# Window attention in a fused Swin and Fourier kernel: the transpose of the attention weights done by VectorE in 32x32 blocks, with the off-diagonal blocks exchanged by SBUF transfers

## The chip, the core and the metric

The kernel runs on one core of a Trainium2 chip. The core has TensorE (PE, matrix multiplies; its weight loads are shown apart as PEld), VectorE (DVE), ScalarE (ACT), GpSimd (POOL) and SyncE (SP), which here only issues DMAs. Each engine works through its own instructions in order and waits on semaphores for the others. The metric is the device time in microseconds from the first to the last instruction. All data are float32.

## What is computed

The input is 32 images of 56 x 56 tokens with 128 channels. Two residual layers follow each other, each behind a group norm (32 groups of 4 channels over the whole image):

```python
x = x + _L0_conv_ref(_gn(x), rpb_table, w_qkv, w_proj, b_proj)   # shifted-window attention
x = x + _L1_conv_ref(_gn(x), w0, w1, W1, b1, W2, b2)             # DCT mixing, then a feed-forward
```

The change lies in the first. The image is rolled by 3 in both directions and cut into 8 x 8 windows of 7 x 7 = 49 tokens. Each window has 4 heads of 32 channels:

```python
attn = jnp.einsum('bhid,bhjd->bhij', q, k)
attn = attn + bias[None]                                    # relative position bias
attn = attn.reshape(B, nW, NH, N, N) + mask[None, :, None]  # shift mask, 0 or -100
attn = jax.nn.softmax(attn.reshape(-1, NH, N, N), axis=-1)
out = jnp.einsum('bhij,bhjd->bihd', attn, v).reshape(-1, N, C)
out = out @ w_proj.T + b_proj
```

The second layer takes a cosine transform along the width and along the height (32 modes each), mixes channels for each mode, transforms back, adds the two, and runs a feed-forward of 128 to 512 to 128 with a relu.

## The kernel before

**Rows.** The unit of work of the attention is a row of 8 windows (7 x 56 tokens); an image has 8 rows, the run has 256. Two windows lie side by side on the 128 partitions, at 0 to 48 and 64 to 112 (JP = 64, WT = 49), so a row has NP = 4 pairs of windows. The score tile `a` holds [128, head, pair, column] for one row; its columns are padded from 49 to 64, and three such tiles rotate.

**What happens to a row.** In its own cycle (a cycle is one pass of the main loop, one row started per cycle): `attn_qk` makes queries and keys, `attn_scores` the scores (TensorE, then VectorE adds bias and mask into `a`, L439), `attn_max` takes the maximum per query (VectorE L449) and subtracts it (GpSimd L450), `attn_v` makes the values, `attn_exp` is the exponential (ScalarE L456), `attn_divide` sums (VectorE L461), takes the reciprocal (L463) and multiplies (GpSimd L464). The weights are now [query, key]; for the product with the values they are needed as [key, query]. `attn_transpose` does that on TensorE against an identity matrix: per pair of pairs and head one transpose of 113 x 113 (PW = 64 + 49 columns hold two windows, so that the result holds the same window pair turned, with columns of other pairs beside it), eight per row, into two PSUM banks; VectorE evacuates one (L485) and ScalarE the other (L483) into tiles `aT`. Three cycles after its own, `attn_values` multiplies with the values (L500, 32 small matmuls), and ScalarE (L533) and VectorE (L531) add the bias while they write `oT`; `attn_project` applies the output weights, VectorE adds the residual (L548), and SP stores the row to a scratch image in DRAM (L554). `attn_sums` prepares the second norm (squares on ScalarE, L570, sums on VectorE).

**Order of work.** TensorE, ScalarE, VectorE and GpSimd follow the order of the program as it is written (a manual schedule); SP's order is laid out by the framework. The main loop lets rows of the attention alternate with the second layer of earlier images: `halves_first` (queries and keys, first half of a feed-forward group), `half_columns` (transforms and mixing), `eighths` (values of row c-3), `quarters` (scores of row c, transforms back), then `attn_max` and `full`, then `halves_last` (values of row c, second half of the feed-forward group, exponential and division of row c, projection of row c-3). `full` transposes in even cycles only, rows c-2 and c-1 together. In even cycles the max of row c stands between these two on VectorE, in odd cycles it stands alone:

```python
for k in (2, 1) if cycle % 2 == 0 else ():
    im, i = row(cycle - k)
    if im:
        attn_transpose(im, i, cycle - k)
    if k == 2 and row(cycle)[0]:
        attn_max(cycle)
next_groups(cycle)
```

In one cycle of eight (row 6 of an image) `next_groups` prepares the next image: 28 transposes on TensorE, and on GpSimd eight additions of a bias (L307) that stand between that row's subtraction and its multiplication. The image's norm (`image_norm`, L334 to L361) follows on VectorE.

**Buffers.** The attention uses four PSUM banks in rotation (`pa`), the second layer four others (`pc`). Tile `res` (two buffers) carries the residual of a feed-forward group: loaded from the scratch image (L745), given its bias on GpSimd (L752), added on VectorE (L788) and stored to the output (L808). Tile `z` (three buffers) takes mixed modes to DRAM (L690), tile `zT` brings them back turned (L701), and `htok` brings columns of the scratch image (L668). Tile `sq` holds the squares and has one buffer of its own.

## Time and profile before

| | |
|---|---|
| timed runs | 3606.96, 3611.10, 3613.36 us (median 3611.1) |
| profiled execution | 3611.8 us, mean granted TensorE clock 0.997 |
| matmuls | 72192, of which 2048 are the transposes of the attention |
| DMA | 390.30 MB, mean 108 GB/s; the queue of SP keeps the 16 DMA engines 39.0% busy |

In the lines of the profile shown below, a group of instructions reads: line of the kernel, engine, operation, output <- inputs, shapes, count | busy time in us, mean ns of one | idle time of its engine just before, and what ended it. Lines of the order of time read: start in us, length in us, engine, line, operation, count, and in brackets the idle time before it with its releaser. PE is TensorE, DVE VectorE, ACT ScalarE, POOL GpSimd, SPq the queue of SP. L112 is the helper through which most matmuls are issued.

### The profile page before, as it was taken

How to read it: one execution, taken by the hardware profiler on the slowest of the kernel's cores; microseconds unless marked ns; L12 is line 12 of the kernel's file. 1: busy time of each engine (PE TensorE's matmuls, PEld its weight loads, DVE VectorE, ACT ScalarE, POOL GpSimd, SP SyncE). 2: the span in 40 equal slices, each digit the busy share in tenths (PEclk: the TensorE clock that was granted, in tenths of full speed). 3: DMA queues.
4: the chain of work that ended last, by engine and by line, in shares of the span. 5: the costliest groups of instructions: out<-in, count | busy, mean ns of one | idle time of the engine just before them, and what ended most of it. 6: DMA issues, size and time to landing. Idle time of an engine off the chain costs nothing.

```text
span 3611.8 us, 161664 instructions
## 1 busy us (share of the span) xinstructions
PE 3552.9 (98%) x72192; PEld 2827.2 (78%) x72192; DVE 2251.9 (62%) x4722; ACT 2145.5 (59%) x4044; POOL 1375.3 (38%) x1437
## 2 busy tenths in 40 slices
PE   7899999999999999999999999999999999999999
PEld 5678787777777787877777787877877878777776
DVE  7766666665666666666656666666666666666641
ACT  5555566665666655666556666556665566655553
POOL 5443343433443433434333434343443344342421
PEclk9999999999999999999999999999999999999999
DMA  4334433444434444343444344443444443444343
GB/s 118 92 102 112 115 106 101 109 112 110 111 98 115 109 109 120 97 110 106 114 106 115 95 111 112 112 117 93 112 108 115 108 112 95 114 109 114 94 115 99
DMA packets 687349, 390.30 MB, mean 108 GB/s; under 512 B 39967, under 2 KB 657600, under 8 KB 686400
## 3 DMA queue, kind: packets, MB, share of 16 engines
q1 hardware_dynamic: 686045, 379.65, 39.0%
q8 instruction: 568, 9.31, 1.1%
q14 instruction: 125, 1.02, 0.1%
q10 hardware_dynamic: 611, 0.32, 0.0%
HBM read 218.29 MB, written 161.48 MB: 105 GB/s over the span
## 4 chain that ended last, share of the span: by engine, by line
PE 93%; DVE 4%; ACT 1%; issue 1%; POOL 1%; DMA 0%; SPq 0%; ACTq 0%; POOLq 0%; DVEq 0%
PE pc L112 38%; PE pa L112 15%; PE pa L409 6%; PE pc L680 6%; PE pa L475 6%; PE pc L646 6%; PE pa L431 5%; PE pa L500 4%; PE pc L719 4%; PE pa L276 1%; PE pc L276 1%; DVE a L439 1%; DVE xf L730 0%; DVE oT L531 0%; POOL rstd L617 0%
## 5 line engine op out<-in xcount | busy, mean ns | idle before, releaser
L450 POOL TENSOR_TENSOR a<-a,mx 128x784 f32<-128x784 f32 x256 | 389.7, 1522 | 1390.7 <-DVE mx L449 966.6
L112 PE MATMUL pc<-wff,hid 128*64 128x128 f32 x12544 | 740.5, 273 | 1.3 <-ACT hid L764 1.0
L112 PE MATMUL pc<-xf,wff 128*64 128x512 f32 (+2 forms) x3584 | 718.3, 539 | 1.1 <-DVE xf L730 1.0
L112 PEld LDWEIGHTS pc<-wff,hid 128*64 128x64 f32 x12544 | 702.7, 137 | 8.0 <-ACT hid L764 4.6
L461 DVE TENSOR_REDUCE sm<-a 128x16 f32<-128x784 f32 x256 | 248.3, 970 | 675.7 <-ACT a L456 669.4
L464 POOL TENSOR_TENSOR a<-a,rs 128x784 f32<-128x784 f32 x256 | 389.6, 1522 | 606.8 <-DVE rs L463 549.4
L764 ACT ACTIVATE hid<-pc,b1sb 128x512 f32<-128x512 f32 (+2 forms) x896 | 522.6, 631 | 71.9 <-PE pc L112 68.9
L112 PEld LDWEIGHTS pc<-xf,wff 128*64 128x64 f32 x3584 | 276.3, 137 | 358.3 <-issue 239.0
L380 ACT ACTIVATE q<-pa,bqkv 128x392 f32<-128x392 f32 x256 | 150.4, 588 | 465.6 <-PE pa L112 459.8
L112 PE MATMUL pa<-xw,wn 128*64 128x392 f32 (+1 forms) x2048 | 390.2, 496 | 10.0 <-ACT wn L364 8.4
L531 DVE TENSOR_SCALAR oT<-pa,bqkv 128x98 f32<-128x98 f32 (+2 forms) x768 | 171.3, 278 | 241.6 <-PE pa L500 241.5
L456 ACT ACTIVATE a<-a 128x784 f32<-128x784 f32 x256 | 222.7, 870 | 146.6 <-POOL a L450 144.6
L752 POOL TENSOR_TENSOR res<-res,b2sb 128x512 f32<-128x512 f32 (+2 forms) x256 | 264.5, 1038 | 113.1 <-DMA res<-scr 105.0
L416 ACT COPY v<-pa 128x512 f32<-128x512 f32 x256 | 151.2, 591 | 244.5 <-PE pa L409 244.3
L307 POOL TENSOR_TENSOR xl<-xl,bproj 112x512 f32<-112x512 f32 (+1 forms) x256 | 287.1, 1143 | 0.0
L409 PE MATMUL pa<-wn,xw 128*64 128x128 f32 x4096 | 283.5, 280 | 3.4 <-ACT oT L533 1.6
L500 PEld LDWEIGHTS pa<-aT,v 49*32 49x32 f32 x16384 | 172.2, 105 | 145.7 <-issue 119.7
L439 DVE TENSOR_TENSOR a<-pa,bm 128x392 f32<-128x392 f32 x512 | 265.0, 560 | 25.8 <-PE pa L431 2.1
L483 ACT COPY aT<-pa 113x452 f32<-113x452 f32 x256 | 139.7, 546 | 208.3 <-PE pa L475 204.7
L449 DVE TENSOR_REDUCE mx<-a 128x16 f32<-128x784 f32 x256 | 246.5, 963 | 4.3
L409 PEld LDWEIGHTS pa<-wn,xw 128*64 128x64 f32 x4096 | 221.0, 137 | 36.0 <-issue 3.1
L788 DVE TENSOR_TENSOR res<-pc,res 128x512 f32<-128x512 f32 (+3 forms) x257 | 138.6, 550 | 175.4 <-PE pc L112 132.8
(97 smaller groups left out, 5746.3 us busy)
## 6 DMA issues: line engine op xcount, KB each, us to landing
zscr<-z SPq DMA_DIRECT2D x512, 112.0 KB
htok<-scr SPq DMA_DIRECT2D x256, 196.0 KB
zT<-zscr SPq DMA_DIRECT2D x192, 256.0 KB
res<-scr SPq DMA_DIRECT2D x160, 256.0 KB
out_dram<-res SPq DMA_DIRECT2D x160, 256.0 KB
scr<-xl SPq DMA_DIRECT2D x128, 224.0 KB
xl<-in_x_dram SPq DMA_DIRECT2D x32, 784.0 KB
xl<-in_x_dram SPq DMA_DIRECT2D x32, 672.0 KB
```

The lines of the kernel that those rows point to most:

```text
L112: nc.tensor.matmul(dst[ps], lhsT=lhsT[:, ps], rhs=rhs, start=start, stop=stop)
L307: nc.gpsimd.tensor_tensor(piece, piece, bproj.unsqueeze(1).to_broadcast([TC, e - a, C]), ALU.add)
L409: nc.tensor.matmul(pv[hs, j * C : (j + 1) * C], lhsT=im.xw[i][:, w * WT : w * WT + JP], rhs=im.w[:, 2 * C : 3 * C], start=True, stop=True,)
L439: nc.vector.tensor_tensor(a[:, 2 * hp : 2 * hp + 2, :, 0:WT].rearrange("p u w j -> p w u j"), ps[hp][:, :RT].rearrange("p (w u j) -> p w u ...
L449: nc.vector.tensor_reduce(mx, a3, axis=AX.X, op=ALU.max)
L450: nc.gpsimd.tensor_tensor(a3, a3, mx.unsqueeze(2).to_broadcast([P, 2 * NWR, WT]), ALU.subtract)
L456: nc.scalar.activation(a3, a3, AF.Exp)
L461: nc.vector.tensor_reduce(sm, a3, axis=AX.X, op=ALU.add)
L464: nc.gpsimd.tensor_tensor(a3, a3, rs.unsqueeze(2).to_broadcast([P, 2 * NWR, WT]), ALU.mult)
L500: nc.tensor.matmul(po4[u][h * HD : (h + 1) * HD, 2 * f + e], lhsT=v[ks, 2 * f + e, h * HD : (h + 1) * HD], rhs=im.aT[i][f][ks, h, e * JP : ...
L752: nc.gpsimd.tensor_tensor(res[:m, c0:c1], res[:m, c0:c1], b2sb[:m].unsqueeze(1).to_broadcast([m, c1 - c0, C]), ALU.add,)
L764: nc.scalar.activation(hf[:, :n], ph[:, :n], AF.Relu, bias=b1sb[:, f : f + 1])
```

## The change

The transposes on TensorE, their two PSUM banks per row and the two evacuations are gone. Instead:

- The score tiles are dense (49 columns, not 64), and two rotate instead of three.
- `attn_divide` multiplies the row twice, once into `own_sb` and once into `off_sb`, each with its 49 columns cut into two blocks: 0 to 31, and 32 to 48 in a block of 32. These are four GpSimd instructions over 128 x 512, 128 x 272, 128 x 512 and 128 x 272 elements. Both tiles exist once.
- Four DMAs from SP then copy, within each window's 64 partitions, the off-diagonal blocks of `off_sb` over those of `own_sb`: second block of the first 32 partitions from the first block of the second 32, and the other way round (32 partitions x 2 KB each).
- `attn_transpose` is one VectorE instruction per row that turns every 32 x 32 block of `own_sb` in place of its partitions and writes `eT` (128 x 1024 elements, two buffers). With the blocks exchanged, that is the whole transpose.
- In the main loop the max of row c stands first in every cycle, then the transpose of row c-1 follows on VectorE, then `next_groups`. Rows are no longer transposed in twos.
- `attn_values` reads `eT`; the windows are numbered so that a pair is two neighbours, and the pieces written to `oT` are runs of 7 tokens instead of 14 with the same number of elements.
- `sq` has no buffer of its own any more and takes one of the three of `z`.

In SP's order the four exchange DMAs of a row stand ahead of that cycle's last store of the output, the store of the row and the load of the next feed-forward group.

```diff
@@ -41,7 +41,7 @@
 QS = HD ** (-0.5)
 FF_GROUPS = (HB, HB, HB, HB, HB, 320, 256)
 FF_AT = (8, 9, 10, 12, 13, 14, 15)
-PW = JP + WT
+KB = 32
 CONV_BEGIN = NWR + 3
@@ -241,11 +241,12 @@
         nc.vector.memset(heads[h * HD : (h + 1) * HD, h % 2 : h % 2 + 1], 1.0)
     q_sb = big.tile([P, RT + JP - WT], F32, tag="q", name="q")
     nc.gpsimd.memset(q_sb, 0.0)
-    v_sb, a_sb = [], []
-    for i in range(3):
-        v_sb.append(big.tile([P, NWR // 2, C], F32, tag=f"v{i}", name=f"v{i}"))
-        a_sb.append(big.tile([P, NH, NP, JP], F32, tag=f"a{i}", name=f"a{i}"))
-        nc.gpsimd.memset(a_sb[i], 0.0)
+    v_sb = [big.tile([P, NP, C], F32, tag=f"v{i}", name=f"v{i}") for i in range(3)]
+    a_sb = [big.tile([P, NH, NP, WT], F32, tag=f"a{i}", name=f"a{i}") for i in range(2)]
+    own_sb = big.tile([P, 2, NH * NP, KB], F32, tag="own_blocks", name="own_blocks")
+    off_sb = big.tile([P, 2, NH * NP, KB], F32, tag="off_blocks", name="off_blocks")
+    nc.gpsimd.memset(own_sb, 0.0)
+    nc.gpsimd.memset(off_sb, 0.0)
@@ -258,7 +259,7 @@
         im.b = b
         im.half = b not in xls
         im.x = load_image(b, 1) if im.half else xls.pop(b)
-        im.xw, im.aT = {}, {}
+        im.xw, im.eT = {}, {}
         im.st = small.tile([P, NWR, 6], F32, tag="st0", name="st0", bufs=2)
         im.part = small.tile([TC, 2, C // 4, NWR], F32, tag="part", name="part", bufs=1)
         im.scr = dram.tile([S, S, C], F32, tag="scr", name="scr", bufs=2)
@@ -403,9 +404,9 @@
         pv = attn_bank()
 
 
-        for w in (0, 2, 1, 3, 4, 6, 5, 7):
-            hs = HALVES[w // 2 % 2]
-            j = w // 4 * 2 + w % 2
+        for w in range(NWR):
+            hs = HALVES[w % 2]
+            j = w // 2
             nc.tensor.matmul(
                 pv[hs, j * C : (j + 1) * C],
                 lhsT=im.xw[i][:, w * WT : w * WT + JP],
@@ -417,7 +418,7 @@
 
     def attn_scores(im, i, r):
 
-        q, a = q_sb, a_sb[r % 3]
+        q, a = q_sb, a_sb[r % 2]
@@ -444,7 +445,7 @@
             )
 
     def attn_max(r):
-        a3 = a_sb[r % 3].rearrange("p t w j -> p (t w) j")[:, :, 0:WT]
+        a3 = a_sb[r % 2].rearrange("p t w j -> p (t w) j")
         mx = small.tile([P, 2 * NWR], F32, tag="mx", name="mx")
         nc.vector.tensor_reduce(mx, a3, axis=AX.X, op=ALU.max)
         nc.gpsimd.tensor_tensor(
@@ -452,38 +453,33 @@
         )
 
     def attn_exp(r):
-        a3 = a_sb[r % 3].rearrange("p t w j -> p (t w) j")[:, :, 0:WT]
-        nc.scalar.activation(a3, a3, AF.Exp)
+        a2 = a_sb[r % 2].rearrange("p t w j -> p (t w j)")
+        nc.scalar.activation(a2, a2, AF.Exp)
 
     def attn_divide(r):
-        a3 = a_sb[r % 3].rearrange("p t w j -> p (t w) j")[:, :, 0:WT]
+        a3 = a_sb[r % 2].rearrange("p t w j -> p (t w) j")
         sm = small.tile([P, 2 * NWR], F32, tag="sm", name="sm")
         nc.vector.tensor_reduce(sm, a3, axis=AX.X, op=ALU.add)
         rs = small.tile([P, 2 * NWR], F32, tag="rs", name="rs")
         nc.vector.reciprocal(rs, sm)
-        nc.gpsimd.tensor_tensor(
-            a3, a3, rs.unsqueeze(2).to_broadcast([P, 2 * NWR, WT]), ALU.mult
-        )
-
-    def attn_transpose(im, i, r):
-
-        a = a_sb[r % 3]
-        im.aT[i] = []
-        for hf in range(2):
-            pt = attn_bank()
-            for h in range(NH):
-                nc.tensor.transpose(
-                    pt[:PW, h * P : h * P + PW],
-                    a[:PW, h, 2 * hf : 2 * hf + 2].rearrange("p w j -> p (w j)")[:, :PW],
-                    ident[:PW, :PW],
+        for dst in (off_sb, own_sb):
+            for k, (j0, n) in enumerate(((0, KB), (KB, WT - KB))):
+                nc.gpsimd.tensor_tensor(
+                    dst[:, k, :, :n],
+                    a3[:, :, j0 : j0 + n],
+                    rs.unsqueeze(2).to_broadcast([P, 2 * NWR, n]),
+                    ALU.mult,
                 )
-            aT = work.tile([P, 4, P], F32, tag="aT", name="aT", bufs=4)
-            src = pt[:PW].rearrange("p (m x) -> p m x", x=P)[:, :, :PW]
-            if hf:
-                nc.scalar.copy(aT[:PW, :, :PW], src)
-            else:
-                nc.vector.tensor_copy(aT[:PW, :, :PW], src)
-            im.aT[i].append(aT)
+        for p in range(0, P, JP):
+            lo, hi = slice(p, p + KB), slice(p + KB, p + JP)
+            nc.sync.dma_start(own_sb[lo, 1], off_sb[hi, 0])
+            nc.sync.dma_start(own_sb[hi, 0], off_sb[lo, 1])
+
+    def attn_transpose(im, i):
+
+        eT = work.tile([P, NH * NP, JP], F32, tag="eT", name="eT")
+        nc.vector.transpose(eT.rearrange("p t (k j) -> p k t j", k=2), own_sb)
+        im.eT[i] = eT
 
     def attn_values(im, i, r):
@@ -492,18 +488,18 @@
         po = [attn_bank(), attn_bank()]
         HALF = RT // 2
         po4 = [p[:, :HALF].rearrange("p (r n s) -> p n r s", r=WS, s=WS) for p in po]
-        for f in range(2):
-            for e in range(2):
-                for h in range(NH):
-                    for u in range(2):
-                        ks = slice(u * JP, u * JP + WT)
-                        nc.tensor.matmul(
-                            po4[u][h * HD : (h + 1) * HD, 2 * f + e],
-                            lhsT=v[ks, 2 * f + e, h * HD : (h + 1) * HD],
-                            rhs=im.aT[i][f][ks, h, e * JP : e * JP + WT],
-                            start=True,
-                            stop=True,
-                        )
+        eT = im.eT.pop(i)
+        for pr in range(NP):
+            for h in range(NH):
+                for u in range(2):
+                    ks = slice(u * JP, u * JP + WT)
+                    nc.tensor.matmul(
+                        po4[u][h * HD : (h + 1) * HD, pr],
+                        lhsT=v[ks, pr, h * HD : (h + 1) * HD],
+                        rhs=eT[ks, h * NP + pr, :WT],
+                        start=True,
+                        stop=True,
+                    )
 
         if i % 2 == 0:
             im.oT = work.tile([P, 2 * RT], F32, tag="oT", name="oT")
@@ -512,19 +508,18 @@
 
         oTr = oT[:, i % 2 * RT : (i % 2 + 1) * RT].rearrange("p (r x) -> p r x", x=S)
         for u in range(2):
-            src = po[u][:, :HALF].rearrange("p (r f x) -> p r f x", r=WS, f=2)
-            x0 = SS + u * 2 * WS
-            if not u:
-                dst = bass.AP(
-                    oTr.tensor, oTr[:, :, x0:].offset, [oTr.ap[0], [S, WS], [4 * WS, 2], [1, 2 * WS]]
-                )
-                parts = [(dst, src)]
-            else:
-                n = S - 4 * WS - x0
-                parts = [
-                    (oTr[:, :, x0 : x0 + 2 * WS], src[:, :, 0]),
-                    (oTr[:, :, S - n : S], src[:, :, 1, :n]),
-                    (oTr[:, :, 0:SS], src[:, :, 1, n:]),
+            src = po[u][:, :HALF].rearrange("p (r f x) -> p r f x", r=WS, f=NP)
+            n = NP - u
+            dst = bass.AP(
+                oTr.tensor,
+                oTr[:, :, SS + u * WS :].offset,
+                [oTr.ap[0], [S, WS], [2 * WS, n], [1, WS]],
+            )
+            parts = [(dst, src[:, :, :n])]
+            if u:
+                parts += [
+                    (oTr[:, :, S - WS + SS :], src[:, :, n, : WS - SS]),
+                    (oTr[:, :, 0:SS], src[:, :, n, WS - SS :]),
                 ]
             for d, f in parts:
                 if u:
@@ -566,7 +561,7 @@
             op=ALU.add,
         )
         yield
-        sq = work.tile([P, 4, C], F32, tag="sq", name="sq", bufs=1)[:TC, : n1 - n0]
+        sq = work.tile([P, 4, C], F32, tag="z", name="sq", bufs=3)[:TC, : n1 - n0]
         nc.scalar.activation(sq, piece, AF.Square)
         nc.vector.tensor_reduce(
             im.part[:, 1, :, i],
@@ -915,15 +910,10 @@
         if im:
             attn_values(im, i, cycle - 3)
 
-    def full(cycle):
-
-        for k in (2, 1) if cycle % 2 == 0 else ():
-            im, i = row(cycle - k)
-            if im:
-                attn_transpose(im, i, cycle - k)
-            if k == 2 and row(cycle)[0]:
-                attn_max(cycle)
-        next_groups(cycle)
+    def turn(cycle):
+        im, i = row(cycle)
+        if im:
+            attn_transpose(im, i)
 
     def next_groups(cycle):
         b, i = divmod(cycle, NWR)
@@ -973,9 +963,7 @@
         im3, i3 = row(cycle - 3)
         if im3:
             attn_values(im3, i3, cycle - 3)
-        im2, i2 = row(cycle - 2)
-        if im2:
-            attn_transpose(im2, i2, cycle - 2)
+        turn(cycle - 2)
         if cycle:
             attn_divide(cycle - 1)
         if im:
@@ -1004,10 +992,9 @@
             start_stats(im3)
             for _ in attn_sums(im3, i3):
                 pass
+            turn(cycle - 1)
             attn_exp(cycle)
             attn_divide(cycle)
-            last, j = row(cycle - 1)
-            attn_transpose(last, j, cycle - 1)
 
     ET = mybir.EngineType
     with tc.manual_schedule(engines={ET.PE, ET.Activation, ET.DVE, ET.Pool}):
@@ -1036,9 +1023,10 @@
                 quarters(cycle)
                 if not has_ff(cycle):
                     next(norm, None)
-                if row(cycle)[0] and cycle % 2:
+                if row(cycle)[0]:
                     attn_max(cycle)
-                full(cycle)
+                turn(cycle - 1)
+                next_groups(cycle)
                 halves_last(cycle, norm)
             b, i = divmod(cycle, NWR)
             if i == (NWR - 2 if b else NWR - 3) and b + 1 < NB:
```

## The prediction

> **What bounds the kernel now.** I read the page from the top: busy shares first, then the chain of work that ended last.
>
> ```profile
> PE 3552.9 (98%) x72192; PEld 2827.2 (78%) x72192; DVE 2251.9 (62%) x4722; ACT 2145.5 (59%) x4044; POOL 1375.3 (38%) x1437
> ...
> PE 93%; DVE 4%; ACT 1%; issue 1%; POOL 1%; DMA 0%; SPq 0%; ACTq 0%; POOLq 0%; DVEq 0%
> PE pc L112 38%; PE pa L112 15%; PE pa L409 6%; PE pc L680 6%; PE pa L475 6%; PE pc L646 6%; PE pa L431 5%; PE pa L500 4%; PE pc L719 4%; PE pa L276 1%; PE pc L276 1%; DVE a L439 1%; DVE xf L730 0%; DVE oT L531 0%; POOL rstd L617 0%
> ```
>
> TensorE sets the end. From 40 to 3460 us it is busy 3385.7 of 3420 us (busy time by stretches), so the other engines matter only where they make it wait. The transposes, L475, are about 6% of the chain. Next, the groups that the change touches, by line:
>
> ```profile
> L475 PE MATMUL pa<-ident,a 113*113 113x113 f32 x2048 | 241.5, 270 | 3.6 <-DVE a L439 1.8 <-ACT k L393 0.4 <-issue 0.4
> L485 DVE COPY aT<-pa 113x452 f32<-113x452 f32 x256 | 159.0, 621 | 37.1 <-PE pa L475 37.1
> L483 ACT COPY aT<-pa 113x452 f32<-113x452 f32 x256 | 139.7, 546 | 208.3 <-PE pa L475 204.7
> L464 POOL TENSOR_TENSOR a<-a,rs 128x784 f32<-128x784 f32 x256 | 389.6, 1522 | 606.8 <-DVE rs L463 549.4 <-ACT bqkv L387 49.2 <-ACT q L380 4.7
> L461 DVE TENSOR_REDUCE sm<-a 128x16 f32<-128x784 f32 x256 | 248.3, 970 | 675.7 <-ACT a L456 669.4 <-ACT bqkv L379 5.7
> ```
>
> The last row shows where VectorE has room: between the max and the sum of a row it idles for the exponential, 669.4 us over 247 waits, 2.7 us a row. Matmuls overlap, so I take the price of the transposes from their place in the order of time, two rows' worth at once:
>
> ```profile
> 1595.67 1.71 PE L719 MATMUL pc<-idcth,zT 64*64 64x112 f32 x64
> 1597.31 1.84 PE L475 MATMUL pa<-ident,a 113*113 113x113 f32 x16
> 1599.08 1.09 PE L409 MATMUL pa<-wn,xw 128*64 128x128 f32 x16
> ```
>
> From start to next start it is 1599.08 - 1597.31 = 1.77 us for 16.
>
> **What the Trainium skill says.** "VectorE: DVE Perf Modes", The three transpose paths: VectorE transposes 32x32 blocks only, and its result goes to SBUF. The page has no float32 price; the small transposes of this trace (below) give one. "DMA: Bandwidth & Descriptors", Anatomy of one DMA, puts about 2.0 us of fixed cost on a DMA, most of it the receipt of the write. The one SBUF-to-SBUF transfer of this trace agrees: 2.43 us from issue to the first VectorE instruction that it released.
>
> ```profile
> 22.89 0.80 SPq L173 DMA_DIRECT2D rpb<-rpb  x1
> ...
> 25.32 1.48 DVE L191 TENSOR_TENSOR bm<-rpb,mask 49x98 f32<-49x98 f32 x8 [1.30 <-DMA rpb<-rpb]
> ```
>
> "GPSIMD Engine Reference", Key points: GpSimd shares SBUF interfaces with VectorE, and contends with its instructions that have two SBUF inputs. The trace agrees: L340, beside a running GpSimd multiply, takes 1295 ns where its like, L341, takes 192. The transposes keep their time (L337 ran beside a GpSimd add).
>
> ```profile
> L340 DVE TENSOR_TENSOR turned<-turned,gmeans 128x32 f32<-128x32 f32 x32 | 41.5, 1295 | 1.1
> L344 DVE STREAM_TRANSPOSE back<-gmeans 128x64 f32<-128x64 f32 x32 | 7.9, 246 | 1.1
> L337 DVE STREAM_TRANSPOSE turned<-stat 128x32 f32<-128x32 f32 x32 | 6.8, 212 | 1.1
> L341 DVE TENSOR_TENSOR turned<-turned 128x32 f32<-128x32 f32 x32 | 6.1, 192 | 1.1
> ```
>
> **The change, part by part.** There are 256 rows, so 128 pairs.
>
> TensorE loses the transposes: 128 x 1.77 = 227 us, on the path. Ends: the chain's 5.9%, 213 us, and the group's busy 241 us. I take 227. The loads L475 and the two evacuations go with them (ACT 140 us, DVE 159 us), all beside TensorE's work: nothing.
>
> VectorE gains one transpose of 1024 elements per row. From 32 to 64 elements it grows 34 ns, 1.06 ns an element: 212 + 992 x 1.06 = 1.27 us, or 325 us in all. VectorE goes to 2252 - 159 + 325 = 2418 us, 71% of a 3400 us run. It stands right after the max, in the 2.7 us gap named above, so 1.27 us is hidden. High end: strided blocks at twice the price, 2.5 us, just fill the gap.
>
> GpSimd multiplies twice over 784 elements in four instructions instead of once in one. L191 takes 375 ns for 98 elements and L464 1522 for 784: 1.67 ns an element, so 1.07 us for 512 and 0.67 for 272; 2 x 1.74 = 3.5 us against 1.5, with ends 3.0 (two L464) and 5. GpSimd goes to 1375 + 256 x 2.0 = 1880 us, 55%. Over a row it is hidden; what it delays comes next.
>
> SP gains four transfers of 64 KB a row, 67 MB, 17% more traffic; the DMA engines would go from 39% to about 46%. An issue takes 0.41 us (four of L690 in 1.64), so the last starts 1.23 us after the first and lands 2.43 later: T = 3.7 us for the exchange. Ends: 2.5, and 7 with a store's 3.8 us and a full queue ahead of it.
>
> The new wait: VectorE's transpose of row c stands behind the max of row c+1 and waits for the exchange. Behind it on VectorE are sum, reciprocal and the additions that give PSUM banks back to TensorE. From the end of a max to the end of the reciprocal is 3.9 us (1613.4 to 1617.3); with 0.2 + 3.5 for GpSimd and T it lands 11.3 us after its own max. It costs nothing until the next max plus 2.6 - 1.27 = 1.3 us. The eight maxes from 1502.15 to 1612.44 are 13.8 us apart in the mean, 12.9 without the transposes: deadline 14.2 in the mean. The shortest step, 12.1 us into row 0, becomes about 10.5, since its max stood 1.07 us behind a copy that goes: deadline 11.8, met barely. Row 6 of each image misses it, because GpSimd first adds a bias to the next image:
>
> ```profile
> 1578.93 2.25 POOL L307 TENSOR_TENSOR xl<-xl,bproj 112x512 f32<-112x512 f32 x2
> 1581.13 1.54 POOL L464 TENSOR_TENSOR a<-a,rs 128x784 f32<-128x784 f32 x1
> ...
> 1587.83 1.52 POOL L450 TENSOR_TENSOR a<-a,mx 128x784 f32<-128x784 f32 x1 [1.97 <-DVE nb L361]
> ```
>
> The multiply starts about 0.5 us earlier than 1581.1 (its max is no longer behind a copy), ends 3.5 later, and the exchange lands at 1587.8. The next max ends at 1587.4 - 1.8 = 1585.6, deadline 1586.9: 0.9 us late, and L340 can wait up to 2 us longer for GpSimd. Once per image, 1 to 3 us on VectorE, and TensorE has 1 to 3 us of banks ahead of it: I take 0.6 us for 31 images, 20 us; ends 0 and 60.
>
> SP's own queue: the result store, the store of the row and the load for the next group now stand behind the exchange, about 5 us later (3.7 + 1.6). The load at 1511.13 served an addition at 1521.21; with some 4 us to land, 6 us were spare. Loads of modes are issued 14 us ahead of use. Hidden: nothing. Squares taking a buffer of the transform's ring: the transfers that free it are a row old, nothing. The column order of windows and 7-element runs leave element counts as they are.
>
> Sum, against this execution's own 3611.8 us: 3611.8 - 227 + 20 = 3405. The timed runs are 3607.0 to 3613.4, median 3611.1, so 0.7 us apart.
>
> **Rivals.** First: the exchange is late in the short rows too. With T = 5.7 instead of 3.7 five rows in eight miss by 0.2 to 2 us, some 5 us an image on VectorE; if 3 reach TensorE, 31 x 3 = 95 us: about 3500. A transpose of 3 us leads to the same. For it: a margin of only 0.3 us in the shortest row; against: 3 us in the mean row.
>
> Second, slower: the exchange becomes a loop that sets the row. Transpose 1.27, sum and reciprocal 1.2, handovers 0.4, multiplies 3.7, then T: 6.6 + T per row. It decides over today's 13.8 us from T = 7.2; at T = 7.7 the row is 14.3, 0.5 x 250 more: about 3735. For it: SP issues in order, and 46% busy engines queue; against: 2.43 measured, and nothing ahead of the exchange in SP's order waits for later work than it does.
>
> Third, no change: the matmuls left take up the time through bank waits, 3611. Against: only a few tens of us of TensorE waits in the whole run.
>
> **How the numbers follow.** Forecast 3405, 60%, own range 3370 (241 us gained) to 3445 (60 us of waits). First rival 25%, third 3%, slower 12%. The low end is 3370; to leave no more than 2 in 10 outside, the high end takes in most of the first rival: 3510. About 0.2% is what a measurement of this kernel can tell. Faster 0.85, same 0.03, slower 0.12.
>
> **What would show it.** No TensorE transposes and a share of 97 to 98%; VectorE transposes at 1.27 us; four multiplies of 3.5 us a row; exchange waits ahead of the transpose only in the row after the bias adds. Wrong if the transpose waits in most rows, or TensorE falls below 95%.

## The result, and the profile after

| | before | after |
|---|---|---|
| timed runs, median | 3611.6 us | 3552.4 us (3548.3 to 3560.7) |
| ratio | | 0.984, 95% interval 0.9824 to 0.9855 |
| profiled execution | 3611.8 us | 3546.4 us, mean granted clock 0.988 |

The change gained 59 us where 206 were forecast: the sign is right, the time lies outside the range. The page of the kernel after, its busy shares (part 1), two rows of its 40 slices (part 2) and the chain of work that ended last (part 4):

```profile
PE 3361.2 (95%) x70144; PEld 2637.0 (74%) x70144; DVE 2494.9 (70%) x4722; ACT 1992.9 (56%) x3788; POOL 1827.4 (52%) x2204
...
PE   4689999999999999999999999999999999999999
...
PEclk8799999999999999999999999999999999999999
...
PE 45%; POOL 17%; DVE 13%; issue 10%; DMA 7%; ACT 4%; SPq 4%; POOLq 0%; DVEq 0%; ACTq 0%
```

The 2048 matmuls are gone, but TensorE's share fell to 94.8% (the page rounds it), and the chain is no longer TensorE's: 93% of it before, 45% now. A chain that ends last can follow any of several branches that are nearly as late, so I do not price anything from these shares; but they say that TensorE has company. The slices (88.7 us each) tell where to look first: three at the start in which TensorE is not full, two of them with a lower granted clock. The same rows of before:

```profile
PE   7899999999999999999999999999999999999999
...
PEclk9999999999999999999999999999999999999999
```

The groups that answer to those shown of before (line engine operation, output <- input, count | busy, mean ns of one | idle time ahead and what ended it):

```profile
L467 POOL TENSOR_TENSOR off_blocks<-a,rs 128x512 f32<-128x512 f32 (+1 forms) x512 | 430.0, 861 | 644.7 <-DVE rs L464 441.6
...
L481 DVE STREAM_TRANSPOSE eT<-own_blocks 128x1024 f32<-128x1024 f32 x256 | 317.5, 1240 | 190.5 <-DMA own_blocks<-off_blocks 175.9
L467 POOL TENSOR_TENSOR own_blocks<-a,rs 128x512 f32<-128x512 f32 (+1 forms) x512 | 430.1, 862 | 0.0
L462 DVE TENSOR_REDUCE sm<-a 128x16 f32<-128x784 f32 x256 | 246.6, 963 | 254.2 <-ACT a L457 253.4
```

Each operation has its forecast price: the transpose 1.24 us (forecast 1.27), the four multiplications 860 us in 256 rows, 3.4 us a row (3.5). The idle time ahead of the sum, 669 us before, is 253: the transpose did move into the gap named for it. What the sum had for one row of each image only stands in the last column of L481: VectorE waits 175.9 us for the exchange, in 110 rows. The lists of waits (engine, line <- what it waited for: us in total, times, longest):

```profile
DVE eT L481 <- DMA own_blocks<-off_blocks: 175.9, 110, 23.8
...
PE pa L112 <- DVE part L566: 28.4, 30, 1.4
PE pa L112 <- DVE nb L362: 22.8, 29, 1.7
PE pa L496 <- DVE eT L481: 19.9, 1, 19.9
```

and of before, the longest wait of TensorE and the only one for `part`:

```profile
PE pa L112 <- ACT wn L364: 8.4, 2, 5.1
...
PE pa L112 <- DVE part L571: 2.0, 2, 1.1
```

Three waits of TensorE are new at this size: for a partial sum of the second norm (`part`), for a result of the first norm (`nb`), and once for the first transpose.

**Where in the run.** The start of the max of row r on VectorE makes a clock for the comparison. Row 17 starts its max at 175.6 us before and at 225.2 after: 49.7 us lost. From row 24 on an image takes 110.62 us before and 106.62 after: 4.0 gained an image, where the removed transposes are worth 4 x 1.77 = 7.1. So there are two losses to find, one in the first rows, one in each image.

### The profile page after: what moved, and what is told of

Read it like the earlier page. It is cut to its first block, busy times and chain, and to the rows that moved or that the text cites. A ratio compares the mean times of both kernels' runs of the same rounds, so it can differ in the third digit from the quotient of the medians.

```text
span 3546.4 us, 159605 instructions
## 1 busy us (share of the span) xinstructions
PE 3361.2 (95%) x70144; PEld 2637.0 (74%) x70144; DVE 2494.9 (70%) x4722; ACT 1992.9 (56%) x3788; POOL 1827.4 (52%) x2204
## 3 DMA queue, kind: packets, MB, share of 16 engines
q1 hardware_dynamic: 735197, 446.82, 49.8%
## 4 chain that ended last, share of the span: by engine, by line
PE 45%; POOL 17%; DVE 13%; issue 10%; DMA 7%; ACT 4%; SPq 4%; POOLq 0%; DVEq 0%; ACTq 0%
PE pc L112 19%; PE pc L641 6%; PE pa L112 5%; POOL own_blocks L467 5%; POOL off_blocks L467 4%; DMA own_blocks<-off_blocks 4%; DVE sm L462 4%; PE pa L410 3%; POOL xl L308 3%; PE pc L675 3%; PE pa L432 3%; POOL a L451 2%; ACT a L457 2%; PE pa L496 2%; SPq L475 2%
## 5 line engine op out<-in xcount | busy, mean ns | idle before, releaser
L467 POOL TENSOR_TENSOR off_blocks<-a,rs 128x512 f32<-128x512 f32 (+1 forms) x512 | 430.0, 861 | 644.7 <-DVE rs L464 441.6
L759 ACT ACTIVATE hid<-pc,b1sb 128x512 f32<-128x512 f32 (+2 forms) x896 | 515.0, 632 | 69.3 <-PE pc L112 67.5
L112 PEld LDWEIGHTS pc<-xf,wff 128*64 128x64 f32 x3584 | 286.0, 137 | 349.2 <-issue 223.2
L481 DVE STREAM_TRANSPOSE eT<-own_blocks 128x1024 f32<-128x1024 f32 x256 | 317.5, 1240 | 190.5 <-DMA own_blocks<-off_blocks 175.9
L467 POOL TENSOR_TENSOR own_blocks<-a,rs 128x512 f32<-128x512 f32 (+1 forms) x512 | 430.1, 862 | 0.0
L112 PE MATMUL pa<-xw,wn 128*64 128x392 f32 (+1 forms) x2048 | 397.5, 503 | 18.6 <-ACT wn L365 9.2
L526 DVE TENSOR_SCALAR oT<-pa,bqkv 128x147 f32<-128x147 f32 (+2 forms) x768 | 171.0, 279 | 219.5 <-PE pa L496 219.5
L496 PEld LDWEIGHTS pa<-eT,v 49*32 49x32 f32 x16384 | 174.6, 106 | 167.5 <-issue 125.6
L112 PE MATMUL pa<-wproj,oT 128*48 128x128 f32 (+1 forms) x3584 | 251.5, 276 | 10.7 <-ACT oT L528 7.3
```

What stands on the lines that cost most here:

```text
L112: nc.tensor.matmul(dst[ps], lhsT=lhsT[:, ps], rhs=rhs, start=start, stop=stop)
L467: nc.gpsimd.tensor_tensor(dst[:, k, :, :n], a3[:, :, j0 : j0 + n], rs.unsqueeze(2).to_broadcast([P, 2 * NWR, n]), ALU.mult,)
L481: nc.vector.transpose(eT.rearrange("p t (k j) -> p k t j", k=2), own_sb)
L496: nc.tensor.matmul(po4[u][h * HD : (h + 1) * HD, pr], lhsT=v[ks, pr, h * HD : (h + 1) * HD], rhs=eT[ks, h * NP + pr, :WT], start=True, sto ...
L759: nc.scalar.activation(hf[:, :n], ph[:, :n], AF.Relu, bias=b1sb[:, f : f + 1])
```

## The experiments

The theory after the comparison had four parts: (a) TensorE does not set the end everywhere, so that its 227 us were never there in full; (b) the second multiplication on GpSimd costs more than "hidden"; (c) the exchange costs in the first rows, not in the later ones; (d) VectorE's transposes cost nothing. The rival to each was that its loss lies in another of the four. The medians (kernel before, timed beside them: 3610.9 to 3614.9):

| kernel | median us | ratio to before, 95% interval |
|---|---|---|
| no_transpose | 3443.9 | 0.9523 to 0.9551 |
| one_multiply | 3447.0 | 0.9524 to 0.9553 |
| no_exchange | 3487.0 | 0.9640 to 0.9669 |
| no_exchange_bias | 3445.3 | 0.9523 to 0.9552 |
| exchange_from_18 | 3505.4 | 0.9684 to 0.9716 |
| consts_later | 3543.1 | 0.9794 to 0.9823 |
| turn_late | 3526.6 | 0.9742 to 0.9774 |
| bias_later | 3577.7 | 0.9893 to 0.9926 |
| no_transpose_max | 3436.8 | 0.9495 to 0.9526 |
| no_transpose_max_k | 3436.1 | 0.9501 to 0.9530 |
| best1 | 3468.2 | 0.9583 to 0.9612 |
| best2 | 3471.4 | 0.9593 to 0.9625 |

### How much of the 227 us is there: no_transpose

The transpose is left out altogether: the values are multiplied with the untransposed weights; one multiplication as before, three score tiles. The other edits of the change stay (dense scores, the numbering of the windows and the runs of 7 tokens, the place of the max, `sq` in the ring of `z`).

```diff
-        for dst in (off_sb, own_sb):
...
+        nc.gpsimd.tensor_tensor(
+            a3, a3, rs.unsqueeze(2).to_broadcast([P, 2 * NWR, WT]), ALU.mult
+        )
...
-        for p in range(0, P, JP):
...
-        nc.vector.transpose(eT.rearrange("p t (k j) -> p k t j", k=2), own_sb)
...
+        eT = a_sb[r % 3].rearrange("p t w j -> p (t w) j")
```

> Leaves the transpose of the attention weights out altogether: the values are multiplied with the untransposed weights, one GpSimd multiply per row, no exchange, no VectorE transpose. What TensorE's 2048 transposes were worth, by itself. Price as in the prediction (1.77 us a pair of rows): 3385 us (3375 to 3400). If the price was the error, that is if the matmuls left take up the time, 3450 or more.

Measured 3443.9: 167 us below before, not 227. Part (a) holds: 60 us were not to be had by this change, however cheap the new transpose. What the edits that stay cost is within the 60 and was not taken apart; VectorE's writes of `oT`, in shorter runs now, take 171.3 us in both kernels. Some 37 of the 60 show as idle time of TensorE. Its row in the stretch from 180 to 3300 us (columns: stretch, its length, then busy us and count of PE, PEld, DVE, ACT, POOL; clock, DMA share, GB/s), of before:

```profile
180.00:3300.00 3120.00, 3104.11 (x63638) 2479.97 (x63632) 1990.72 (x4156) 1881.19 (x3547) 1200.54 (x1238) 1.00 0.40 108
```

and of no_transpose, with its wait for the second norm's partial sum:

```profile
180.00:3300.00 3120.00, 3067.05 (x64938) 2425.34 (x64936) 2000.75 (x4110) 1835.53 (x3488) 1250.57 (x1296) 1.00 0.43 114
...
PE pa L112 <- DVE part L551: 28.7, 30, 1.4
```

TensorE idles 53 us there instead of 16. The profile of before held the hint. In its order of time, the last partial sum of a norm and the matmul that reads it:

```profile
1522.09 0.68 DVE L571 TENSOR_REDUCE part<-sq 112x32 f32<-112x512 f32 x1
...
1522.82 0.43 PE L112 MATMUL pa<-part,gmean 112*64 112x64 f32 x4
```

The sum ends at 1522.77 and the matmul starts at 1522.82. These 0.05 us are not room to spare: in no_transpose, where TensorE idles for this sum, the matmul starts 0.06 us after it too. So the sum already released TensorE, in 24 of the 32 images of before (0.05 to 0.06 us each), and the list of waits shows next to nothing of it, because the matmul ahead is recorded as ending later than that (at 1522.90 here). Shorten TensorE's work ahead of this point, and it waits, 0.96 us in each of 30 images of no_transpose. Per image 5.42 us are gained (110.62 to 105.20), 1.66 fewer than 7.08; over the 29 images after row 24 that is 48. The first 24 rows give 12.9 us (271.1 to 258.2) where 24 x 0.885 = 21.2 were due: TensorE is not full there before either (busy 121.8 of the 140 us from 40 to 180).

### VectorE's transposes and the second multiplication: one_multiply, no_exchange, no_exchange_bias

no_exchange leaves the four DMAs out of the changed kernel, one_multiply the multiplication into `off_sb` as well:

```diff
-        for dst in (off_sb, own_sb):
-            for k, (j0, n) in enumerate(((0, KB), (KB, WT - KB))):
-                nc.gpsimd.tensor_tensor(
-                    dst[:, k, :, :n],
...
-        for p in range(0, P, JP):
...
+        for k, (j0, n) in enumerate(((0, KB), (KB, WT - KB))):
+            nc.gpsimd.tensor_tensor(
+                own_sb[:, k, :, :n],
```

> The changed kernel with the four exchange transfers of a row left out (only the diagonal blocks are right); multiplies and VectorE transposes stay. Theory A, the exchange is late (first rows and later rows): 3400 to 3430, what is left being the norm held up by GpSimd. Theory B, the doubled GpSimd work holds VectorE and the row up: only the 24 us wait and part of the slow first rows come back, 3480 to 3500.

> The changed kernel without the exchange (as no_exchange) and with one multiply per row on GpSimd in two instructions, the off-diagonal copy left out; the VectorE transposes stay. no_exchange took 3487, no_transpose 3444. If the doubled multiplies are what is left between them (they hold up VectorE's norm): 3455 (3445 to 3465). If it is the VectorE transposes: 3480 to 3490.

one_multiply took 3447.0, no_exchange 3487.0. Against no_transpose, VectorE's 256 transposes (316 us of its time) cost 3 us, which is less than these medians can tell from nothing: part (d) holds. The second multiplication costs 40 us although GpSimd is busy for half of the run only. By rows, the step from row 6 to row 7 takes 17.89 us with it and 16.62 without; the other seven steps of an image differ by 0.6 or less in either direction (an image in all: 106.12 against 105.11; the first 24 rows lose another 8.6 us). That is the row in which the next image's bias is added. In the order of time of the kernel after, in an image in which it shows most, GpSimd first:

```profile
1579.29 2.25 POOL L308 TENSOR_TENSOR xl<-xl,bproj 112x512 f32<-112x512 f32 x2
1581.49 1.68 POOL L467 TENSOR_TENSOR off_blocks<-a,rs 128x512 f32<-128x512 f32 x2
1583.13 1.68 POOL L467 TENSOR_TENSOR own_blocks<-a,rs 128x512 f32<-128x512 f32 x2
```

then VectorE, in the norm of the next image, and TensorE, which needs that norm:

```profile
1579.64 0.18 DVE L323 TENSOR_REDUCE gsums<-turned 128x8 f32<-128x32 f32 x1
1579.86 4.98 DVE L326 TENSOR_SCALAR gmeans<-gsums 128x32 f32<-128x32 f32 x1
1584.88 0.19 DVE L341 TENSOR_TENSOR turned<-turned,gmeans 128x32 f32<-128x32 f32 x1
...
1591.36 0.28 PE L112 MATMUL pa<-nb,wqkv 128*64 128x1 f32 x4 [1.45 <-DVE nb L362]
```

L326 scales 32 elements and takes 4.98 us; its like 6 us later takes 0.18. It ends at 1584.84, 0.03 us after the last of GpSimd's multiplications (1584.81). Everything behind it on VectorE, scores, max and `nb`, comes later by as much. This is one of the longest. The group in before, after and one_multiply (it runs twice an image, and only the first is held up for long):

```profile
L325 DVE TENSOR_SCALAR gmeans<-gsums 128x32 f32<-128x32 f32 x64 | 23.8, 372 | 2.2
```

```profile
L326 DVE TENSOR_SCALAR gmeans<-gsums 128x32 f32<-128x32 f32 x64 | 96.7, 1511 | 2.2
```

```profile
L326 DVE TENSOR_SCALAR gmeans<-gsums 128x32 f32<-128x32 f32 x64 | 57.7, 901 | 2.2
```

Of 29 images of the kernel after in which it takes over 1 us, it takes 4.7 to 5.0 in four and 2.1 to 2.7 in the other 25, and there the next two instructions, L341 and L342, are held up too. The three together take 4.3 us in the median image, in no_exchange as well, and 3.3 in one_multiply. The difference, 1.0 us, is as much as an image loses by the second multiplication. The Trainium skill has a mechanism that fits ("SBUF — State Buffer", Who interferes with whom): a VectorE `tensor_scalar` can run in a mode that takes the ports shared with GpSimd, and then one of the two blocks fully. The prediction had looked only at instructions with two SBUF inputs. The page says that the loser is blocked for the length of the other's instruction. Here it lasted longer: in the 25 images L326 let two of GpSimd's instructions end and came through at the end of the third, in the four at the end of the whole queue.

no_exchange_bias tests this: no_exchange, with the bias additions taken out of row 6.

```diff
-        if im.b > 1:
-            image_bias(im, i)
...
+            b, i = divmod(cycle, NWR)
+            if b > 1 and i in (0, 1, 4, 5):
+                image_bias(images[b], 2 * (i % 4 + i // 4 * 2))
```

> The four exchange DMAs are left out (the values are multiplied with weights whose off-diagonal blocks are not exchanged), and the next image's bias is added in rows 0, 1, 4 and 5 instead of row 6; both GpSimd multiplications and VectorE's transposes stay. no_exchange took 3487, the same with one multiplication 3447. Theory A, the 40 us between them lie in row 6, where bias additions and two multiplications stand one behind the other on GpSimd and hold up VectorE's norm (its L326 takes 5 us): 3445 to 3460, and the mean of that group falls from 1518 ns to below 500. Theory B, they lie in all rows, or in the first rows, because GpSimd takes 1.9 us longer everywhere: 3475 or more, although the group gets shorter.

3445.3 us, and the group of L326 is as short as a free one:

```profile
L324 DVE TENSOR_SCALAR gmeans<-gsums 128x32 f32<-128x32 f32 x64 | 13.3, 208 | 2.2
```

The step from row 6 to row 7 is 14.36 us, the one after it 11.96 instead of 9.16: the two together are 26.32, as in one_multiply, against 27.05. Both multiplications are still there, and the 40 us are gone: what the second one cost was its place behind the additions and ahead of the norm, not its 1.7 us a row. (In the first 24 rows some 6 us remain against one_multiply, and an image takes 104.98 us against 105.11. The edit was not tried on one_multiply; TensorE idles only 0.03 us an image in these two rows there, so they had little left to give. The edit takes the additions away from row 6's own multiplication as well as from the norm, so that the ports have the whole of the effect is argued from the sizes, not shown.)

An earlier version of the same edit, on the changed kernel and with the additions in rows 0 to 3 (`if b > 1 and i < NWR // 2`), had made it slower:

> The changed kernel with the next image's bias additions moved from row 6 (ahead of its multiplies on GpSimd) to rows 0 to 3 of the image itself, behind their multiplies. Theory A (exchange late in the rows after): row 6's exchange comes earlier, but row 7's, the late one, stays: 3530 (3515 to 3550). Theory B (GpSimd, which stands busy through the norm, holds VectorE's norm up by 5 us and TensorE by 1.5 to 2.5 us an image): 3480 to 3500.

3577.7, 25 us above the changed kernel; neither theory had that. The stall of L326 went (208 ns), but in rows 2 and 3 the second norm is made, by small VectorE instructions (`own`, `nm`, `ve`, `shift`) and one of GpSimd (`rstd`), and additions now run beside them: `nm` takes 1012 ns in the mean instead of 419 and `ve` 1033 instead of 173, and from the end of `own` to the start of `shift` it is 3.6 us in the median instead of 1.6. The waits of bias_later from 180 to 3250 us (the first is 9.0 us in the whole run of the changed kernel):

```profile
PE pc L639 <- DVE xf L723: 58.8, 28, 2.4
...
DVE shift L612 <- POOL rstd L610: 30.6, 28, 1.8
```

The step from row 2 to row 3 went from 13.53 to 15.49 us. Rows 2 and 3 are those of the partial sum that TensorE already waits for (above), so the additions went to rows 0, 1, 4 and 5 in the runs after it.

### Where the exchange costs: consts_later, turn_late, exchange_from_18

no_exchange lies 65 us below the changed kernel. Only the first 18 rows without exchange:

```diff
-        for p in range(0, P, JP):
...
+        if r >= 18:
+            for p in range(0, P, JP):
...
```

> The changed kernel with the four exchange DMAs left out in the first 18 rows only (their weights stay without the exchanged blocks); from row 18 on everything is as in the changed kernel, exchange waits of VectorE included. The exchange as a whole costs 65 us (3552 against 3487). Theory A, most of that lies in the first rows, where the exchange stands behind constant loads and closes a loop with the next row: 3495 to 3510, and row 17 starts its max near 178.5 us instead of 225. Theory B, the loss is one of the later rows, where VectorE waits 115 us in sum for the exchange, and the first rows only shift it: 3530 or more.

3505.4 us, and row 17 starts its max at 179.5 us: 47 of the 65 us lie in the first 18 rows and 18 in the other 238, although VectorE still waits for it 95 times from 330 us on, 121 us in sum. Part (c) holds. The first rows of the changed kernel in order of time, the queue of SP first:

```profile
46.17 7.29 SPq L134 DMA_DIRECT2D b2sb<-in_b_dram  x1
53.56 0.62 SPq L475 DMA_DIRECT2D own_blocks<-off_blocks  x1
```

then VectorE:

```profile
34.59 0.97 DVE L450 TENSOR_REDUCE mx<-a 128x16 f32<-128x784 f32 x1
59.40 1.25 DVE L481 STREAM_TRANSPOSE eT<-own_blocks 128x1024 f32<-128x1024 f32 x1 [23.83 <-DMA own_blocks<-off_blocks]
...
69.02 1.25 DVE L481 STREAM_TRANSPOSE eT<-own_blocks 128x1024 f32<-128x1024 f32 x1 [4.77 <-DMA own_blocks<-off_blocks]
...
78.74 1.25 DVE L481 STREAM_TRANSPOSE eT<-own_blocks 128x1024 f32<-128x1024 f32 x1 [2.70 <-DMA own_blocks<-off_blocks]
```

The first exchange stands in SP's order behind the loads of the second image and of all constants, and VectorE stands 23.8 us. After that the transposes come every 9.6 us (rows 1 to 10). This is the loop of the second rival, 6.6 + T: transpose, sum, reciprocal, multiplications, exchange, transpose. From the start of a transpose to the end of the next row's multiplications it is 5.8 us, and from there to the next transpose, T, 3.4 to 4.6. A row of the main loop takes 13.8 us, so there it fits in the mean; but rows 2 to 8 have no second layer yet to fill the time, and took 7.5 us each before (8.3 in no_exchange). Of the 49.7 us that row 17 is late, 21.6 are lost by the max of row 2, 12.1 from there to row 8, and 16.0 in the nine rows after it, where the second layer begins. And TensorE, with gaps in its work, is granted less clock. From 100 to 180 us it is 0.73, against 0.96 before (columns as above):

```profile
100.00:180.00 80.00, 56.81 (x1156) 41.22 (x1158) 54.91 (x110) 32.54 (x59) 46.48 (x51) 0.73 0.39 88
```

The Trainium skill tells why a gap costs twice ("TensorE: Matmul & The Clock Gate", Part 1: the clock is halved when TensorE has been idle for a while). The trace agrees as far as it goes; what the clock alone is worth of the 47 us no run separates.

Two edits try to win the loss back with the whole computation. consts_later issues half of the second image, the mixing and the feed-forward weights in pieces between the first 11 rows; turn_late has two `own_sb` and one `eT`, and transposes row c-2 instead of c-1 (in the first rows, row c-2 after the division instead of ahead of it), so that an exchange has a row more.

```diff
-        xls[1] = load_image(1)
-    w1sb = const_load([P, NM, C], w1, "w1sb")
...
+        xls[1] = load_image(1, 0)
...
+        load_late(cycle)
```

```diff
+        own_sb = owns[r % 2]
...
-                turn(cycle - 1)
+                turn(cycle - 2)
                 next_groups(cycle)
```

> The changed kernel with the loads of the second image and of the second layer's constants (5.6 MB) issued in pieces over the first ten rows instead of ahead of the first row's exchange. Theory A: the 24 us wait of the first transpose goes, the loop of the first rows (9.5 us a row) stays: 3525 (3510 to 3535). Theory B: the waits of the first rows come from GpSimd, 3550.

> The changed kernel with two buffers for the own blocks and the VectorE transpose of a row one row later, so that an exchange has a whole row more. The whole computation is done. If lateness of the exchange is worth the 65 us between the change and no_exchange, apart from the 24 us that the first one waits behind the loads: 3510 (3500 to 3525). If it is the traffic or SP's time and not the wait: 3545 or more.

consts_later gained 9 us (3543.1), turn_late 26 (3526.6); both fell short of what was expected. Both start the max of row 17 some 17 to 18 us earlier (207.3 and 208.6 instead of 225.2). consts_later keeps the loop, and its images take 107.11 us instead of 106.62. In turn_late the exchange makes VectorE wait only once:

```profile
DVE eT L485 <- DMA own_blocks<-off_blocks: 19.5, 1, 19.5
```

Its images still take 106.76 us, 0.6 more than without an exchange. So the small part of the exchange's price, the 18 us of the later rows, is not VectorE's wait for it alone. By rows it has two places. The step from row 7 to the next row 0 takes 9.43 us in the changed kernel and 9.16 in no_exchange: this step is shorter than the loop, the transpose waits just ahead of `nb`, and TensorE waits 22.8 us for `nb` instead of 14.7. turn_late wins this back (9.16 us; 15.0). The step from row 4 to row 5 takes 13.73 us instead of 13.37, and 14.13 in turn_late, with pauses in some of the images in which TensorE stops amid a group of matmuls and the profile shows nothing that it waits for:

```profile
PE pc L645 <- issue: 9.9, 7, 2.9
```

That is the largest such entry of turn_late, 8.4 us of it in this row of the 28 full images after row 24; no_exchange has no such pause there. What they are stays open. The additional 0.5 us of consts_later lies in the same two steps (14.01 and 9.63).

### What holds the rest: no_transpose_max, no_transpose_max_k

Is it VectorE's work in rows 2 and 3 that keeps 60 us from no_transpose? First the max was put ahead of the additions to `xf`; then, in these two rows, the second half of the keys was given to ScalarE.

```diff
             attn_scores(im, i, cycle)
+            if cycle >= CONV_BEGIN:
+                attn_max(cycle)
...
-                if row(cycle)[0]:
-                    attn_max(cycle)
```

```diff
-            attn_qk(im, i, False)
+            attn_qk(im, i, i in (2, 3))
```

> no_transpose (3444) with the max of a row put ahead of the additions of the transform back on VectorE in rows 2 and 3. Theory: 1.0 to 1.7 us an image are lost because TensorE's matmul for the second norm's sums stands at the end of the chain additions, max, subtraction, exponential, sum, partial sums, which was as long as TensorE's work before; shortened by the 2.2 us of the additions it frees TensorE: 3405 (3395 to 3420). If VectorE is simply full there: 3435 to 3445.

> no_transpose_max (transpose left out as a whole, max ahead of the xf additions) with the second half of the keys written by ScalarE instead of VectorE in rows 2 and 3 of each image, so VectorE has one instruction less in the two rows whose end its chain sets. Theory A, VectorE's work in rows 2 and 3 is what keeps the removal of TensorE's transposes from its full 227 us: 3437 falls to 3410 to 3422, and the waits of TensorE for the xf additions (26.5 us in 27 waits) fall below 8. Theory B, it is a matter of order or of ScalarE as well: 3430 or more, the wait has another name.

3436.8 and 3436.1: 7 us for the order, nothing for the lighter VectorE. The wait only changed its name, and then stayed. Of no_transpose_max and of no_transpose_max_k:

```profile
PE pc L626 <- DVE xf L710: 26.5, 27, 1.2
```

```profile
PE pc L626 <- DVE xf L710: 25.5, 24, 1.2
```

That does not show that the amount of VectorE's work is without effect, for the lighter load had a price: ScalarE, with the keys ahead of its squares, delivers these later, and VectorE waits for them 58 times, which it does not in no_transpose_max:

```profile
DVE part L551 <- ACT sq L550: 59.0, 58, 1.4
```

The order of time of no_transpose_max_k ahead of one such wait, VectorE and then TensorE:

```profile
1442.32 0.69 DVE L551 TENSOR_REDUCE part<-sq 112x32 f32<-112x512 f32 x1 [1.17 <-ACT sq L550]
1444.24 0.27 DVE L576 SCALAR_TENSOR_TENSOR own<-pa,gavg 128x64 f32<-128x64 f32 x1 [1.24 <-PE pa L112]
...
1445.82 0.16 DVE L599 SCALAR_TENSOR_TENSOR shift<-ms,rstd 128x1 f32<-128x1 f32 x1 [0.66 <-POOL rstd L597]
...
1449.09 3.49 PE L626 MATMUL pc<-dct_w,xl 112*64 112x64 f32 x112 [1.14 <-DVE xf L710]
```

VectorE itself waits three times in these 6 us: for ScalarE's squares, for TensorE's averages, for GpSimd's power (`rstd`). It is a chain of handovers through four engines, the second norm, with the scores, max and `xf` additions behind it. That a shorter chain would bring the 60 us is argued from these lines; no run shortened it, and none lightened VectorE without loading another engine of the chain.

### The parts together: best1, best2

best1 has the whole computation, with turn_late, consts_later, the bias in rows 0, 1, 4 and 5, and the max ahead of the additions; best2 adds the keys by ScalarE in rows 2 and 3.

> All together, the whole computation: transpose one row later with two buffers, constants loaded late, bias additions in rows 0, 1, 4 and 5, max ahead of the additions. If the three losses (first rows, norm, sums of the second norm) are apart and add: 3420 (3400 to 3440). If one is shadowed by another that then shows: 3460 to 3500.

> The whole computation: best1 with the same edit (second half of the keys by ScalarE in rows 2 and 3). If VectorE's chain in these rows is what best1 has left above TensorE's own work (31.0 us in 30 waits for the xf additions): 3440 to 3450. If the exchange or ScalarE takes the place of that wait: 3460 to 3470, no different from best1.

best1 took 3468.2 us, faster than both kernels: 4.0% below before, 84 us below the changed kernel. The edits do not add up as if apart (3420 was expected). It reaches 104.98 us an image, as good as without any exchange (104.98 in no_exchange_bias, which lacks the edit of the max). What it has left over that kernel is in the first rows: row 17 at 191.1 us against 175.9. best2 is no different (3471.4), like no_transpose_max_k beside no_transpose_max.

## Why the prediction was wrong

The runs make a ladder in which each step adds one part (medians; a step is uncertain by some 5 us):

| step | us | forecast |
|---|---|---|
| the transposes leave TensorE (before to no_transpose) | -167 | -227 |
| VectorE transposes, two score tiles (to one_multiply) | +3 | 0 |
| second multiplication (to no_exchange) | +40 | hidden; norm in the 20 below |
| exchange from row 18 on (to exchange_from_18) | +18 | +20 |
| exchange in the first 18 rows (to the changed kernel) | +47 | 0 |
| sum | -59 | -207 |

- **"TensorE loses the transposes: 128 x 1.77 = 227 us, on the path."** This step failed by 60 us: with the transposes gone and nothing in their place, 167 us were gained. That TensorE was busy 3385.7 of 3420 us shows that it hardly waited; it does not show how far the others are behind it, and at the partial sum of the second norm they were not behind it at all. The third rival (the matmuls left take up the time through waits) was set aside because there were "only a few tens of us of TensorE waits in the whole run". That list cannot tell: it holds the waits at today's speed. It happened for a quarter of the sum. How much of it is the second norm's chain is not shown; TensorE's waits for `part` are 28.7 us of it.
- **"1.27 us is hidden"**, in the 2.7 us gap before the sum: right, in price (1.24) and in effect (3 us).
- **"Over a row it is hidden"**, of GpSimd's 2 us a row: right for all rows but one, and the first 24 rows, where some 6 us remain (no_exchange_bias). For row 6 the prediction named the mechanism, "L340 can wait up to 2 us longer", and gave the whole of row 6, late exchange included, 0.6 us an image. The term was mis-sized: 40 us over the run, 1.0 us an image and 8.6 us in the first 24 rows. The instruction that stood longest was L326, which the prediction did not look at: 2.7 us in most images, 5 in some. The profile of before had it already, with a mean of 372 ns for what takes 180 alone.
- **T = 3.7 us, with ends 2.5 and 7.** Measured from the end of the second multiplication to the start of the transpose, in the 96 rows from 250 us on in which VectorE waited: median 4.7, a tenth of them above 7.5 (these are the late rows; where it did not wait, the landing is not seen). An issue took 0.58 us in the median (forecast 0.41, read from a store; the eight transfers between SBUF tiles at the start of before had taken 0.76 to 0.88). So T in these rows lies between forecast and first rival, the transposes waited in 110 rows (forecast: 31), and yet the later rows lost 18 us. That this is close to the forecast's 20 is luck: the forecast had it in the rows after the bias additions alone. The first rival came nearer to the waits (five rows in eight; measured 3.4) and had their price, 95 us, wrong: in exchange_from_18 VectorE waits 121 us and the run loses 18.
- **"It decides over today's 13.8 us from T = 7.2."** This step put the first rows at nothing, and they lost 47 us: the failure that the order of time of the first rows would most easily have spared. The loop 6.6 + T was worked out, and nearly right: 5.8 + 3.4 to 4.6 in rows 1 to 10. It was compared only with a mean row of the main loop. Rows 2 to 8 of the run take 6 to 8.5 us each and were never looked at; and of SP's order I asked only what the exchange delays, not what stands ahead of it. The sentence "nothing ahead of the exchange in SP's order waits for later work" is true and beside the point: ahead of the first one stand the constants' loads, issued up to 53.5 us.
- **What would show it.** Multiplications and transposes came as said. Of the two signs of failure that were named, waits in most rows did not come (110 of 256) and TensorE below 95% did, just (94.8%); the kernel was faster all the same.

## What to carry to other kernels

An engine that is 98% busy sets the end only as far as the next chain is behind it: before pricing what is taken off it, look in the order of time for instructions that end just before it reads them. Where its own instruction starts one handover after such an end (0.05 us here), it already waits, though no list shows it, and nothing is to be gained ahead of that point. A new loop (A waits for B, B for the next A) has to be held against the shortest row of the run, start-up included, not the mean one. Work moved to an engine that is half idle is free only where nothing queued behind it is due, and where no small instruction of another engine needs ports that it holds.

## What the runs showed of the hardware

- A VectorE `tensor_scalar` of 128 x 32 float32 from SBUF to SBUF takes 0.18 us alone. Beside a queue of GpSimd additions and multiplications it took 2.1 to 2.7 us in 25 images of the kernel after, up to the end of the third of their instructions, and 4.7 to 5.0 in four, up to the end of the queue. Ahead of the longest, from 1578.4 to 1579.9 us, beside the additions, a VectorE reduction (L323, 0.18 us), a transpose of 128 x 32 (L338, 0.21 us) and a `tensor_scalar` that reads PSUM (L398, 0.68 us) kept their times.
- The exchange, four transfers of 64 KB each between partitions of SBUF, took 4.7 us in the median and up to 8.8, from the last multiplication to the transpose, in the 96 later rows in which VectorE waited for it, and 3.4 to 4.6 in rows 1 to 10. The transfer of `rpb` in the kernel before had taken 2.4 from its issue. The queue of SP keeps the DMA engines 49.8% busy instead of 39.0%; that the longer times come from that was not tested.
- A float32 transpose by VectorE of 128 x 1024 in 32 x 32 blocks takes 1.23 to 1.25 us in all 256 rows, beside GpSimd or not.
